# The causal mask of a gated attention moved into free rows of a bf16 product's operands

## The chip, the cores and the metric

The kernel runs on one core of a Trainium2 chip. A core has five engines with their own queues: TensorE (PE; its weight loads are shown as PEld), VectorE (DVE), ScalarE (ACT), GpSimd (POOL) and SyncE (SP, which here only issues DMAs), and 16 DMA engines. The metric is the device time of one execution in microseconds, as a median over runs. Times inside an execution come from one profiled execution and count from its first instruction.

## The reference

The input x is 8 sequences of 256 tokens with 512 features (2048 tokens); a context of the same shape is given. Two layers follow each other, each with an attention and a feed-forward part:

- layer 0: a retention-like attention over the context, then a feed-forward part whose weights are ternary and whose activations are rounded to 8 bits;
- layer 1: a matrix-LSTM attention with 16 heads of 32 features, then a mixture of 32 experts (4 of them for each token) with one shared expert.

The change is in layer 1's attention. Cut to what matters, for each batch and head:

```python
log_f_cum = concat([0, cumsum(log_sigmoid(fg))])
fg_mat    = log_f_cum - log_f_cum.T
log_D     = where(ltr, fg_mat[1:, 1:], -inf) + ig.T      # ltr: key not after query
D         = exp(log_D - max(log_D, -1))
C         = (q @ k.T / sqrt(32)) * D
Cn        = C / (maximum(abs(C.sum(-1)), exp(-max_log_D)) + 1e-6)
h         = Cn @ v                                       # then a norm per head
```

So each head needs a 256 by 256 matrix of exponentials of a sum of a term of the key and a term of the query, with everything where the key comes after the query set to zero.

## The kernel before, in words

The tokens lie in 16 tiles of 128. `layers_joined` (L1095) runs layer 0's feed-forward over the 16 tiles t and starts layer 1's attention behind it; between `layer0_attention` and it, `layer1_constants` (L654) builds constants. In both the order of PE, ACT, DVE, POOL and SP is the order in which the code emits (a manual schedule). Each engine takes its instructions in that order, and one that waits holds all behind it.

**A tile of the feed-forward** (t = 0 to 15) does: `products(t, n)` for three column blocks on PE (L1116), `silu` on ACT (L1124), `gated` on DVE (L1129), the row maximum `largest` (L1133), `shifted` (L1142), the rounding `hidden_rounded` (L1155, or L1153 on ACT) with a transposing DMA on SP (L1157), `input_rounded(t + 2)` (L1182, tile xq) with another (L1184), `output(t - 2)` (L1163), `added` (L1168) and `stats` (L127). Work of layer 1's gates (`Gates`, its generator `chain`) is placed among these by tables `steps`, `places` and `spread`: keys are (round, place in the round), values how many steps of a generator to run there.

**The exponent operands.** The gates leave, in DRAM (`parts_d`), for each row of a batch and head the key's and the query's term as three bf16 parts each, whose sum is the float32 value. For one batch b and one block k of HG = 4 heads, the exponents come from one bf16 product: its stationary operand `left` holds the key terms' three parts for the four heads in rows 0 to 11, and ones in rows 12 to 14; its moving operand `right` holds in rows 0 to 11 a pattern that picks the head, and in rows 12 to 14 the query terms' parts. So 15 rows (KR) of the 128 carry data and the others are zero. `lefts(b)` and `rights(b)` load the data rows on SP (L717, L723); there are two `left` tiles and two `right` tiles, taken in turn by batch. The second `right` is made in `second_right` (L703) in a buffer that held a weight of the feed-forward (in the profile such buffers have the name held): a memset, a copy of 12 rows by a DMA of POOL, then the loading and scaling of `ln_scale` (L711, L712). `layer1_right` (L682) writes the head pattern into the first, one block in each of tiles 2 to 5, on ACT.

**A round.** `layer1_rounds` (L686) goes through 32 blocks (b, k) in rounds n. In round n, `decays` (L736) makes the exponentials xe of block n, `weights` (L762) the product of queries and keys times xe (tile ct, one DVE instruction for two heads, L777) of block n - 1, `heads` (L783) the product with the values of block n - 2, and `back` (L801) brings block n - 3 to rows of tokens (tile hid). `decays` does this in three parts; each is one 512-column product (L749), one product that adds -1e30 to the masked places (L750), and one exponential (L754). The mask product has the identity as its stationary operand and `lateb`, a 128 by 128 triangle, as its moving one, repeated over the heads of the part:

```python
nc.tensor.matmul(pd, lhsT=lhsT, rhs=rhs, start=True, stop=False)
nc.tensor.matmul(
    pd[:, :, :P], lhsT=g.identb, rhs=lateb.unsqueeze(1).to_broadcast([P, CH // n, P]),
    start=False, stop=True,
)
nc.scalar.activation(out, pd, AF.Exp)
```

The first two parts take the first 128 keys with all 256 queries of two heads each, the third the last 128 keys with the last 128 queries of four heads. `pd` has two buffers, xe two and a third in a held buffer (`at["third"]`), which every third block takes.

**The tail of a batch** (`tail`, L885) spreads the norm of a finished batch over rounds n = 6 + 4b + r: r = 0 `scales` (L816, the maximum of |sum| and exp(-max)) and squares, r = 1 `variance` (L831, L832), r = 2 the inverse root, for b up to 5 by `rsqrt_aside` (L108: L113 and L114 on DVE, L115 to L120 on POOL), r = 3 the scaling of the heads (L838) and their addition to x (L845, L846, on POOL for b up to 5; the second half at r = 0 of the next batch), r = 5 and 6 the statistics of the new x (L127, L921, on DVE), which enter the next batch's root, r = 10 to 13 the normed rows (L864, L865) and their transposes (L875).

Of the kernel before, what the change touches and what calls it, by code (L numbers as in the profile page):

```python
# [6 lines left out]

# [645 lines left out]

def layer1_constants(g, wp):  # L654
    nc = g.nc
    g.lateb = wp.tile([P, P], BF16, tag="lateb", name="lateb")
    nc.gpsimd.memset(g.lateb, 0.0)
    nc.gpsimd.affine_select(
        out=g.lateb, in_=g.lateb, compare_op=ALU.is_ge, fill=-1e30, base=0, pattern=[[1, P]], channel_multiplier=-1
    )  # L660
    g.head = wp.tile([P, HG], F32, tag="head", name="head")
    nc.gpsimd.memset(g.head, 0.0)
    for part in range(3):
        nc.gpsimd.affine_select(
            out=g.head, in_=g.head, compare_op=ALU.not_equal, fill=1.0, base=-HG * part, pattern=[[-1, HG]],
            channel_multiplier=1,
        )

    g.left = [wp.tile([P, KD, S], BF16, tag=f"left{n}", name=f"left{n}") for n in range(2)]
    g.right = [wp.tile([P, KD, HG, S], BF16, tag="right0", name="right0")]  # L670
    for left in g.left:
        nc.gpsimd.memset(left, 0.0)
        nc.gpsimd.memset(left[:KR], 1.0)
# [7 lines left out]

def layer1_right(g, k):  # L682
    g.nc.scalar.copy(g.right[0][:, k], g.head.unsqueeze(2).to_broadcast([P, HG, S]))


def layer1_rounds(g, tc, gates, work, ps, qp):  # L686
# [4 lines left out]
    row = 2 * H1 * (HD1 + 1)  # L691
    hid_of, at = [], {}

    def opened(held):
        row = 2 * H1 * (HD1 + 1)
        first = g.ctxT[0].rearrange("p k t -> p (k t)")
        for t in (held[0][:, :row], held[0][:, row : 2 * row], first[:, :row]):
            hid_of.append(t.rearrange("p (j h d) -> p j h d", j=2, h=H1))
        gates.em = held[0][:, 2 * row : 2 * row + 2 * P].rearrange("p (n q) -> p n q", n=2)
        at["third"] = held[1][:, : HG * (S + P)].rearrange("p (r s) -> p r s", r=HG)  # L700
        at["squared"] = held[1][:, HG * (S + P) :][:, : 2 * H1 * HD1]

    def second_right():  # L703
        more = qp.tile([P, NF * D // 2], F32, tag="wq2", name="held2")
        half = KD * HG * S // 2
        nc.gpsimd.memset(more[:, :half], 0.0)
        right = more[:, :half].bitcast(BF16).rearrange("p (k r s) -> p k r s", k=KD, r=HG)
        nc.gpsimd.dma_start(out=right[: 3 * HG], in_=g.right[0][: 3 * HG])
        g.right.append(right)
        g.lns = more[:, half : half + D]  # L710
# [3 lines left out]
    def lefts(b):  # L714

        for part in range(3):
            nc.sync.dma_start(  # L717
                out=g.left[b % 2][HG * part : HG * (part + 1)],
                in_=parts_d[0, part, b * H1 : (b + 1) * H1].rearrange("(k r) s -> r k s", r=HG),
            )  # L720
# [15 lines left out]
    def decays(b, k):  # L736
# [3 lines left out]
        if (b * KD + k) % 3 < 2:  # L740
# [4 lines left out]
        def part(lhsT, rhs, late, out):  # L745
            pd = ps.tile([P, CH], F32, tag="dec", name="pd", bufs=2)
            n = rhs.shape[-1]
            pd = pd.rearrange("p (r s) -> p r s", s=n)
            nc.tensor.matmul(pd, lhsT=lhsT, rhs=rhs, start=True, stop=False)  # L749
            nc.tensor.matmul(  # L750
                pd[:, :, :P], lhsT=g.identb, rhs=lateb.unsqueeze(1).to_broadcast([P, CH // n, P]),
                start=False, stop=True,
            )
            nc.scalar.activation(out, pd, AF.Exp)  # L754

        for r in range(0, HG, 2):
            part(keys[:, :P], rows[:, r : r + 2, :], lateb, xe[:, r : r + 2, :S])
        yield xe
        part(keys[:, P:], rows[:, :, P:], lateb, xe[:, :, S:])
# [41 lines left out]
    def back(x, hid, k):  # L801
# [7 lines left out]
        nc.scalar.copy(hid[:, :, k * HG : (k + 1) * HG, :].rearrange("p j h d -> p j (h d)"), pt)  # L809
# [6 lines left out]
    def scales(b, hid):  # L816
# [3 lines left out]
        nc.scalar.activation(nm, hid[:, :, :, HD1], AF.Abs)  # L820
        nc.vector.tensor_max(nm, nm, gates.em[:, :, b * H1 : (b + 1) * H1])
# [244 lines left out]
    class Rounds:  # L1066
        def second_right(self):
            second_right()

        def lefts(self, b):  # L1070
# [782 lines left out]
```

## Time and profile before

| | us |
|---|---|
| median of 3 runs | 1052.13 (1050.63 to 1052.27) |
| the profiled execution, device time | 1052.05 |
| its span, first to last instruction | 1049.8 |
| layer 0's feed-forward, tiles 7 to 11 | about 281 to 320 |
| rounds of layer 1's attention, first to last exponent product | 358 to 492 |
| busy: PE, PEld, DVE, ACT, POOL | 997.9, 607.5, 530.7, 405.0, 397.7 |
| mean granted clock of TensorE | 0.987 |

How to read what follows. A line of an engine in order of time has the start in us, the length in us, the engine, the line of the code, the operation, output<-inputs, partitions x elements and type, and how many like it follow each other; in brackets, how long the engine had been idle before it and what ended that. Matmuls are pipelined: the next may start before the listed end of the one before. The view of windows gives a stretch's busy time for each engine. The waits give who waited for whom: total us, times, longest. The groups by tile give shortest, median and longest duration in ns.

### The profile page before, as it was taken

The page shows a single profiled execution, that of the slowest core. Times are in us where ns is not written, and L with a number is a line of the kernel's source. Part 1 is how long each engine was busy: PE and PEld are TensorE (multiplying, and loading weights), DVE is VectorE, ACT ScalarE, POOL GpSimd, SP SyncE. Part 2 cuts the span into 40 slices and gives each one's busy share as a digit, 9 for nine tenths or more (in the row PEclk, how much of TensorE's full clock was granted, in tenths as well). Part 3 has the DMA queues.
Part 4 walks back from the last instruction along what each step waited for, and adds up shares of the span by engine and source line. Part 5 has one row for each costly group of instructions (what it writes and reads, how often), then busy time and mean ns, then how long its engine had stood idle before and what let it go on. Part 6 is the DMA issues. An engine that isn't in the chain of part 4 may idle for free.

```text
span 1049.8 us, 14708 instructions
## 1 busy us (share of the span) xinstructions
PE 997.9 (95%) x5210; PEld 607.5 (58%) x5210; DVE 530.7 (51%) x1355; ACT 405.0 (39%) x692; POOL 397.7 (38%) x474
## 2 busy tenths in 40 slices
PE   6999999979999899999998989999999999999995
PEld 5766666534454355666444445556566667777773
DVE  6545566669997858887837941121212221221210
ACT  4453443447677657876421001211222223212121
POOL 0023434450000114888403044544555556545432
PEclk9999999999999999999899989999999999999998
DMA  9664433323332411231211446877877778889983
GB/s 342 228 200 146 140 102 145 101 66 57 71 62 39 90 38 48 70 127 50 76 74 51 150 145 155 211 189 179 209 195 196 209 208 227 225 228 247 235 225 49
DMA packets 101009, 152.39 MB, mean 145 GB/s; under 512 B 39577, under 2 KB 42265, under 8 KB 100893
## 3 DMA queue, kind: packets, MB, share of 16 engines
q1 hardware_dynamic: 81984, 106.78, 32.5%
q0 software_dynamic: 18944, 44.60, 19.4%
q8 instruction: 43, 0.70, 0.3%
q14 instruction: 38, 0.30, 0.1%
HBM read 110.42 MB, written 32.96 MB: 137 GB/s over the span
## 4 chain that ended last, share of the span: by engine, by line
PE 75%; DVE 12%; POOL 4%; ACT 3%; issue 2%; DMA 1%; SPq 0%; POOLq 0%; ACTq 0%; DVEq 0%
PE po L1640 14%; PE pu L1623 13%; PE pg L1623 13%; PE pw L363 5%; PE pz L398 5%; PE pt L1680 3%; PE p L1116 2%; PE pgu L988 2%; DVE am L1133 2%; DVE h L1129 2%; PE pv L297 2%; DVE ct L777 1%; PE s L340 1%; PE pq L331 1%; PE po L379 1%
## 5 line engine op out<-in xcount | busy, mean ns | idle before, releaser
L1628 DVE TENSOR_TENSOR act<-pu,sg 128x264 f32<-128x264 f32 (+22 forms) x68 | 31.8, 468 | 313.3 <-PE pu L1623 300.7
L1665 POOL DMA_INDIRECT xg<-h_d,tok_of x85 | 83.3, 980 | 199.1 <-DVE of L1675 64.3
L1684 POOL DMA_INDIRECT out_x<-eo,to x85 | 133.0, 1564 | 55.1 <-ACT eo L1722 34.4
L1640 PE MATMUL po<-w,act 128*128 128x512 f32 (+10 forms) x456 | 143.1, 489 | 0.0
L1623 PE MATMUL pg<-xT,w 128*128 128x216 f32 (+21 forms) x512 | 134.8, 406 | 0.8 <-issue 0.8
L1722 ACT ACTIVATE eo<-po,slotw 128x512 f32<-128x512 f32 (+10 forms) x114 | 65.6, 576 | 177.0 <-PE po L1640 168.4
L1623 PE MATMUL pu<-xT,w 128*128 128x216 f32 (+21 forms) x512 | 133.3, 403 | 0.0
L1623 PEld LDWEIGHTS pg<-xT,w 128*128 128x128 f32 x512 | 93.2, 190 | 33.2 <-issue 17.8
L1623 PEld LDWEIGHTS pu<-xT,w 128*128 128x128 f32 x512 | 96.8, 190 | 26.2 <-issue 5.6
L1627 ACT ACTIVATE sg<-pg 128x264 f32<-128x264 f32 (+22 forms) x68 | 28.5, 419 | 205.1 <-PE pg L1623 183.4
L1116 PE MATMUL p<-wq,xqT 128*128 128x512 bf16 (+1 forms) x384 | 81.2, 361 | 7.1 <-DVE qi L1137 6.3
L1640 PEld LDWEIGHTS po<-w,act 128*128 128x128 f32 (+10 forms) x456 | 54.1, 154 | 57.4 <-issue 47.9
L384 POOL TENSOR_TENSOR y<-y,gam 128x512 f32<-128x512 f32 x16 | 20.2, 1263 | 139.4 <-DVE y L81 139.4
L1116 PEld LDWEIGHTS <-xqT 128*128 128x128 bf16 x384 | 37.2, 98 | 49.5 <-issue 12.6
L1681 DVE TENSOR_TENSOR xT<-pt,nw 128x512 f32<-128x512 f32 (+12 forms) x85 | 51.0, 600 | 20.5 <-PE pt L1680 20.5
L398 PE MATMUL pz<-wo,wyT 128*128 128x512 f32 x128 | 59.4, 608 | 1.3 <-ACT wyT L393 1.3
L363 PE MATMUL pw<-wg,xnT 128*128 128x512 f32 x128 | 57.8, 594 | 0.0
L1680 PEld LDWEIGHTS pt<-ident,xg 128*128 128x128 f32 (+15 forms) x340 | 39.2, 140 | 23.5 <-PE po L1640 10.5
L127 DVE BATCH_NORM_STATS2 st<-x 128x6 f32<-128x512 f32 x64 | 43.9, 686 | 12.5 <-POOL x L846 6.3
L1680 PE MATMUL pt<-ident,xg 128*128 128x128 f32 (+15 forms) x340 | 47.0, 260 | 0.6 <-DVE xT L1681 0.5
L777 DVE SCALAR_TENSOR_TENSOR ct<-pqk,xe 128x768 f32<-128x768 f32 x44 | 40.0, 950 | 8.4 <-PE pqk L773 7.9
L636 POOL TENSOR_TENSOR sw<-sw 64x256 f32<-64x256 f32 x2 | 1.3, 662 | 111.8 <-ACT sw L629 111.8
(338 smaller groups left out, 1714.9 us busy)
## 6 DMA issues: line engine op xcount, KB each, us to landing
w<-in_w SPq DMA_DIRECT2D x32, 1024.0 KB
w<-in_w SPq DMA_DIRECT2D x32, 512.0 KB
wst<-in_w1T SPq DMA_DIRECT2D x8, 704.0 KB
wst<-in_w3T SPq DMA_DIRECT2D x8, 704.0 KB
wst<-in_w2T SPq DMA_DIRECT2D x6, 768.0 KB
x<-in_x SPq DMA_DIRECT2D x16, 256.0 KB
ctxT<-in_ctxT_d SPq DMA_DIRECT2D x4, 1024.0 KB
raw<-in_ctx SPq DMA_DIRECT2D x16, 256.0 KB
```

Of the source, the lines that this page charges most:

```text
L127: g.nc.vector.bn_stats(st, x)
L363: nc.tensor.matmul(pw, lhsT=xnT[c][:, k, o : o + P], rhs=wg[:, k, :], start=k == 0, stop=k == KD - 1)
L398: nc.tensor.matmul(pz[i], lhsT=wyT[i][:, k, :], rhs=wo[:, k, :], start=k == 0, stop=k == KD - 1)
L777: nc.vector.scalar_tensor_tensor(ct[:, r : r + 2, :], pqk[:, :, : S + P], 1.0 / math.sqrt(HD1), xe[:, r : r + 2, :], ALU.mult, ALU.mult,)
L1116: nc.tensor.matmul(both[:, m, : z - a], lhsT=xqT[:, k, :], rhs=w[:, k, a:z], start=k == 0, stop=k == KD - 1)
L1623: nc.tensor.matmul(pp[:, :n], lhsT=w[:, k, cols], rhs=xT[:, k, :n], start=k == 0, stop=k == KD - 1)
L1640: nc.tensor.matmul(po[h * at : h * at + n, :cols], lhsT=act[:, m, j * P : j * P + n], rhs=w[:, m, h * cols : (h + 1) * cols], start=m == 0 ...
L1665: nc.gpsimd.indirect_dma_start(out=xg[:n], out_offset=None, in_=h_d, in_offset=bass.IndirectOffsetOnAxis(ap=g.tok_of[:n, r, j : j + 1], ax ...
L1680: nc.tensor.transpose(pt[:, k, :n], xg[:n, k * P : (k + 1) * P], g.ident[:n, :n])
L1681: nc.vector.tensor_mul(xT, pt[:, :, :n], g.nw.unsqueeze(2).to_broadcast([P, KD, n]))
L1684: return nc.gpsimd.indirect_dma_start(out=g.out, out_offset=bass.IndirectOffsetOnAxis(ap=rows, axis=0), in_=eo, in_offset=None, compute_op ...
L1722: nc.scalar.activation(eo[:n, at : at + cols], po, AF.Copy, scale=w[r][:n, j : j + 1])
```

## The change

Layer 1's causal mask is no longer added by a 128-column triangle. The rows 15 to 127 of the operands, which were zero, now carry it: in `left`, row p has -1e30 in column p of each block of 128 keys; in `right`, row p has one where p is greater than the query's place in its block. Their product is -1e30 where the key is past the query, for keys from 15 on. For keys below 15 a small triangle of 14 columns is still added by a second product (14 columns for each of 4 heads). The last 128 queries against the first 128 keys need no mask: they take a third stationary operand, `open`, with zeros in rows 15 to 127, of which there are again two by batch, loaded by three more DMAs for each batch.

The rows are built by POOL instructions, three in each of the tiles 7 to 11 of the feed-forward (14 in all), each made to wait for that tile's last silu. ACT copies block 0 of `right` to blocks 1 to 3 in tiles 11 to 13, where before it wrote the pattern in tiles 2 to 5. The second `right` is made by copying rows 0 to 11 and 15 to 127 of the first; it moves to the other held buffer, and the third xe to its place.

The maximum of the norms: hid's rows get one more column; ACT copies exp(-max) into it, and one DVE reduction over pairs with absolute values takes the place of an absolute value on ACT and a maximum of two tiles on DVE. The last steps of the gates' second chain move from round 17 to 18.

```diff
-        for r in range(0, HG, 2):
-            part(keys[:, :P], rows[:, r : r + 2, :], lateb, xe[:, r : r + 2, :S])
+        part(keys[:, :P], rows[:, :, :P], xe[:, :, :P])
+        part(g.open[b % 2][:, k], rows[:, :, P:], xe[:, :, P:S], False)
         yield xe
-        part(keys[:, P:], rows[:, :, P:], lateb, xe[:, :, S:])
+        part(keys[:, P:], rows[:, :, P:], xe[:, :, S:])
...
+            nc.tensor.matmul(pd, lhsT=lhsT, rhs=rhs, start=True, stop=not masked)
+            if masked:
+                few = lateb.shape[-1]
+                nc.tensor.matmul(
+                    pd[:, :, :few], lhsT=g.identb, rhs=lateb.unsqueeze(1).to_broadcast([P, HG, few]),
+                    start=False, stop=True,
+                )
...
-        if (b * KD + k) % 3 < 2:
+        n = b * KD + k
+        if n % 3 or n == 0:
             xe = work.tile([P, HG, S + P], F32, tag="xe", name="xe")
         else:
             xe = at["third"]
...
+def operand_rows(g):
+    nc = g.nc
+    rows = g.right[0][:, 0]
+    yield nc.gpsimd.memset(rows, 0.0)
+    under = rows.rearrange("p r (j s) -> p (r j) s", s=P)
+    yield nc.gpsimd.affine_select(
+        out=under, in_=under, compare_op=ALU.is_ge, fill=1.0, base=0, pattern=[[0, 2 * HG], [1, P]], channel_multiplier=-1
+    )
+    yield nc.gpsimd.memset(rows[:KR], 0.0)
+    for part in range(3):
+        yield nc.gpsimd.affine_select(
+            out=rows, in_=rows, compare_op=ALU.not_equal, fill=1.0, base=-HG * part, pattern=[[-1, HG], [0, S]],
+            channel_multiplier=1,
+        )
+    for left in g.left:
+        yield nc.gpsimd.memset(left, 0.0)
+        blocks = left.rearrange("p k (j t) -> p (k j) t", t=P)
+        yield nc.gpsimd.affine_select(
+            out=blocks, in_=blocks, compare_op=ALU.not_equal, fill=-1e30, base=0, pattern=[[0, 2 * KD], [-1, P]],
+            channel_multiplier=1,
+        )
+        yield nc.gpsimd.memset(left[:KR], 1.0)
+    yield nc.gpsimd.memset(g.open[0], 0.0)
+    yield nc.gpsimd.memset(g.open[0][:KR], 1.0)
...
 def layer1_right(g, k):
-    g.nc.scalar.copy(g.right[0][:, k], g.head.unsqueeze(2).to_broadcast([P, HG, S]))
+    g.nc.scalar.copy(g.right[0][:, k], g.right[0][:, 0])
...
     def second_right():
-        more = qp.tile([P, NF * D // 2], F32, tag="wq2", name="held2")
         half = KD * HG * S // 2
-        nc.gpsimd.memset(more[:, :half], 0.0)
-        right = more[:, :half].bitcast(BF16).rearrange("p (k r s) -> p k r s", k=KD, r=HG)
-        nc.gpsimd.dma_start(out=right[: 3 * HG], in_=g.right[0][: 3 * HG])
+        right = at["held"][:, :half].bitcast(BF16).rearrange("p (k r s) -> p k r s", k=KD, r=HG)
+        for rows in (slice(0, 3 * HG), slice(KR, P)):
+            nc.gpsimd.dma_start(out=right[rows], in_=g.right[0][rows])
         g.right.append(right)
...
+        for part in range(3):
+            nc.sync.dma_start(
+                out=g.open[b % 2][HG * part : HG * (part + 1)],
+                in_=parts_d[0, part, b * H1 : (b + 1) * H1, :P].rearrange("(k r) s -> r k s", r=HG),
             )
...
-        nc.scalar.activation(nm, hid[:, :, :, HD1], AF.Abs)
-        nc.vector.tensor_max(nm, nm, gates.em[:, :, b * H1 : (b + 1) * H1])
+        nc.scalar.copy(hid[:, :, :, HD1 + 1], gates.em[:, :, b * H1 : (b + 1) * H1])
+        nc.vector.tensor_reduce(nm, hid[:, :, :, HD1:], AX.X, ALU.max, apply_absolute_value=True)
...
-                silu(t, 2)
+                last = silu(t, 2)
...
-                if 2 <= t < 2 + KD:
-                    layer1_right(g, t - 2)
+                if 7 <= t < 7 + 5:
+                    behind = last
+                    for ins in itertools.islice(builds, 3):
+                        tc.add_manual_dep(
+                            ins.ins, behind.ins.name,
+                            mybir.DependencyInfo(mybir.DependencyClass.Sync, mybir.DependencyReason.DATA),
+                            reason="each in its tile's time",
+                        )
+                if 10 < t < 10 + KD:
+                    layer1_right(g, t - 10)
...
-                (2, 0): [partial(output, late, "back", 1)],
+                (2, 0): [partial(output, late, "back", 1), rounds.second_right],
                 (2, 1): [partial(added, late), early],
-                (2, 2): [rounds.second_right],
+                (2, 2): [rounds.third],
...
-            spread = {..., (15, 4): 1, (17, 1): 2, (17, 4): 1}
+            spread = {..., (15, 4): 1, (18, 1): 2, (18, 4): 1}
```

`layer1_constants` loses the building of `left` (two memsets each), of the triangle's other 114 columns and of the head pattern (a memset and three selects).

## The prediction

> **What bounds the kernel now.** I read first the windows around the second layer's attention, then the waits by releaser, then single engines in order of time. A round is one pair of batch and block of four heads: 32 in all, four to a batch. PE in round 16 (start us, length us):
>
> ```profile
> 432.46 0.39 PE L749 MATMUL pd<-right,left 128*128 128x512 bf16 x1
> 432.69 0.27 PE L750 MATMUL pd<-lateb,identb 128*128 128x256 bf16 x1
> 432.80 0.38 PE L749 MATMUL pd<-right,left 128*128 128x512 bf16 x1
> 433.01 0.27 PE L750 MATMUL pd<-lateb,identb 128*128 128x256 bf16 x1
> 433.12 0.62 PE L805 MATMUL back<-turn,numT 128*128 128x132 f32 x4
> 433.65 0.38 PE L749 MATMUL pd<-right,left 128*128 128x512 bf16 x1
> 433.86 0.38 PE L750 MATMUL pd<-lateb,identb 128*128 128x512 bf16 x1
> 434.17 0.73 PE L769 MATMUL pqk<-qT,ctxT 32*128 32x256 f32 x8
> ```
>
> Lengths overlap; an instruction's cost is the distance to the next start. The three mask products (lateb) hold PE for 0.11 + 0.11 + 0.31 = 0.53 us of a round of 3.38 us. PE looks full, so it is tempting to count 0.53 thirty-two times. Windows (length, then busy us of PE, PEld, DVE, ACT, POOL, then clock and DMA) and waits (total, times, longest) say otherwise:
>
> ```profile
> 289.00:297.00 8.00, 7.38 (x39) 3.67 (x38) 7.80 (x17) 6.70 (x9) 0.00 (x0) 1.00 0.31 59
> 297.00:305.00 8.00, 8.00 (x44) 4.36 (x43) 7.79 (x20) 6.26 (x9) 0.00 (x0) 1.00 0.38 73
> 369.00:398.00 29.00, 27.54 (x256) 15.46 (x258) 17.40 (x37) 17.28 (x36) 4.53 (x4) 1.00 0.19 52
> 398.00:424.00 26.00, 24.76 (x278) 15.33 (x278) 25.14 (x41) 19.27 (x45) 13.48 (x22) 1.00 0.10 28
> ...
> DVE st L127 <- POOL x L846: 6.3, 5, 1.8
> POOL var L115 <- DVE rsq L113: 5.4, 5, 1.9
> ```
>
> Tiles 7 to 10 of the feed-forward (281 to 313 us) leave DVE no gap while POOL is empty. Rounds 2 to 6 (369 to 398) are PE's: DVE has 17.40 of 29. Rounds 7 to 12 are DVE's (25.14 of 26). From 424 to 497 a loop rules, one turn a batch: POOL takes the root, scales the heads and adds them to x (L115 to L846, 9.6 to 10.2 us in a row); DVE waits for that x in all five batches, then does L127, L831, a ct, L127 and L113 (5.2 us); POOL waits for L113. That makes 14.8 to 15.4; the turns start at 424.61, 439.41, 454.86, 470.72 and 486.95. There is no PE time in it; PE's four rounds need 13.5, with two transposed tiles at 0.44 each 14.4.
>
> **The change part by part.**
>
> *Masks on PE.* Three mask products a round go, two of 56 columns come. By the rows a column costs (0.379 - 0.273)/256 us, so 56 cost 0.02; but the weights of the open product behind the first take 0.097 (PEld row of L750). Between 0.02 and 0.11 for it I take 0.10, nearest the weight row; for the one ahead of pqk, between 0.10 and 0.31, 0.20. A round saves 0.53 - 0.30 = 0.23 (0.11 to 0.41), 7.4 in all rounds. It reaches the end only in rounds 2 to 6, and of these five about one is lost to waits inside (num for DVE's qT 0.89, back for numT 0.41): 4 x 0.23 = **-0.9** (-0.4 to -1.6). Rounds 0 and 1 wait for DMA and ACT; from 7 on DVE and the loop cover the masks. ACT's exponents keep count and size; block 2 writes xe again after block 0's ct (done 370.60, exponent at 370.51): 0.1, in the rounding.
>
> *Maximum of the norms.* ACT's Abs (0.25) becomes a copy of as many elements: nothing. DVE's maximum reads two tiles and took 0.18 beside an idle POOL:
>
> ```profile
> 416.63 1.06 DVE L821 TENSOR_TENSOR nm<-nm,held 128x32 f32<-128x32 f32 x1
> 430.20 1.49 DVE L821 TENSOR_TENSOR nm<-nm,held 128x32 f32<-128x32 f32 x1
> ...
> 429.74 1.91 POOL L838 TENSOR_TENSOR held<-held,rsq 128x1024 f32<-128x1024 f32 x1
> ```
>
> The second ends (430.20 + 1.49) as POOL's L838 ends (431.65). Reductions show no such stretching: L831 takes 1.19 beside POOL and 1.21 without. Only 416.63 lies in the DVE-bound part; there the next stats start 0.45 after POOL's x was ready, so **-0.4** (0 to -0.9). At 430.20 DVE waits for POOL afterwards anyway.
>
> *Operand rows on POOL, tiles 7 to 11.* This is where I expect the loss. 14 instructions, three after each tile's last silu, two in tile 11. Rows of before:
>
> ```profile
> L672 POOL MEMSET left<- x2: 946/954/962, 228.6 to 233.0; 128x1024 bf16 x2
> ...
> L658 POOL TENSOR_SCALAR_AFFINE_SELECT lateb<-lateb x1: 297/297/297, 229.5 to 229.5; 128x128 bf16<-128x128 bf16 x1
> ...
> 294.37 0.42 DVE L1182 TENSOR_SCALAR xq<-xn 128x512 bf16<-128x512 f32 x1
> ```
>
> A select of 4 columns takes 0.19 and of 128 0.30: 0.86 ns a column, so 1024 take 1.07; a memset 0.95. POOL's time itself is free. But silu ends at 285.66, 294.00, 301.83 and 309.83, and xq starts 0.06 to 1.2 us after that, just inside the three. If it is held to the end of the POOL instruction that runs: tile 7 1.1, tile 8 0.75, tile 9 0.9, tile 10 0.85 and 1.05 more for L104 (two inputs, beside the select): 4.7. If only selects hold, 2.3 (0.5 + 0.75 + 0 + 1.05). No row shows DVE beside a memset or select of this size, so 0 to 4.7; L821, L921 (0.62 beside POOL's L865, else 0.17) and L636 (1.24 beside L838, else 0.42) are the nearest rows and all hold: between the two cases **+3.3**. DVE has no gap there, so it passes to the end one for one.
>
> [...]
>
> *Copy in round 2.* The memset of 1.81 goes; a copy of 113 rows of 8 KB joins that of 12 (1.02 MB together). It now goes into the buffer of w3, free when tile 15's products end at 355.5, and POOL has nothing before it: it starts some 17 us earlier than before (memset at 372.55), beside the transposing DMA of hq (issued 356.81), for which PE waits 1.61 us until 360.38. The 16 DMA engines are full from 358 to 361 (windows: share 1.05, 1.01, 0.86 at 205, 180 and 297 GB/s). At these rates the copy takes 3.4 to 5 us. If they share, hq lands up to 3.5 later; 0.56 of it is slack (PE then waits for ACT). 0 to 3, I take **+1.2**. Rights of batch 1 no longer wait on SP for POOL's memset (7.6 us); not needed before 381. The ln_scale multiply (1.52 on POOL at 380.39) comes earlier too, perhaps beside DVE's root chain (363.8 to 365.1), whose end ACT awaits: 0 to 1.5, **+0.4**. The open memsets and DMA issues on POOL (0.6 each) stand in front of nothing urgent.
>
> *SP.* 24 more DMAs of 0.3. In tile 15 three stand ahead of the hq transpose; SP had 0.8 free there: 0.1 at most. Later lefts go out at 425.3, 440.3, 454.6, 469.6 for rounds that start at 432.5 (16), 447.7, 462.7, 478.1: 6 us to spare. Nothing.
>
> *ACT.* Four casts of 1.03 go from tiles 2 to 5, three copies come to tiles 11 to 13. ACT idles after each of them (2.48, 1.23 and 3.24 us); without that cover they'd cost 3. POOL's memsets at 228 to 235 go; that path is DMA Wif (3.71). Nothing. The second gates' last steps move from round 17 to 18: PE's wait of 0.48 for POOL goes, off the loop.
>
> **Sum** against the profiled execution (1052.05; span 1049.8 and 2.25 around it; 0.08 below the median): -0.9 - 0.4 + 3.3 + 1.2 + 0.4 = +3.6, **1055.7**.
>
> **The rivals.**
>
> 1. POOL's rows slip between DVE's instructions and the copy yields to hq: the costs are 0, -1.3 remains, 1050.8. For it: memsets read nothing, and no row shows them holding DVE. Against: xq's place just behind silu. No change that can be told.
> 2. Faster: PE sets the loop's rounds after all and the masks pay in all 32: -7.4 - 0.4 + 4.9 = -2.9, 1049.2 (1044.3 with no costs). It decides once PE rather than POOL's x is what DVE waits for, that is, if the turn gets shorter than 14.8. For it: 72.11 of 76 us busy on PE from 424 to 500. Against: the two waits above, ten times in five batches.
> 3. Much slower: selects take what POOL's two-input rows do (1.18 for 512, so 2.4), and hq is held 3.5: +4.7 + 3.0 + 1.5 - 0.4 = +8.8, 1060.9.
> 4. The short products save nothing beyond 0.11 a round: the masks' term is -0.4, the sum +4.1; inside the forecast.
>
> **How the numbers follow.** This kernel's runs can't tell less than about 0.2%, 2.1 us, from no change. Forecast 0.52, rival 3 0.10 (both slower), rival 1 0.22 (same), rival 2 0.16 (faster). The range leaves out rival 2's end and the top of rival 3: 1050.0 to 1060.0; the forecast's own range is 1054.2 to 1058.5.
>
> **What would show it.** Right: xq at 0.6 to 1.5 us in tiles 7 to 10, the ends of these tiles 2 to 5 us later; hq's landing later than 3.5 us after issue; nm near 0.2 always; round time 3.15 on PE in rounds 2 to 6 but turns of 14.8 to 16 as before, with PE idle before pqk. Wrong: xq at 0.42 throughout; turns under 14.5.

## The result, and the profile after

| | before | after |
|---|---|---|
| median, us | 1052.20 (4 runs, 1050.63 to 1052.50) | 1065.09 (4 runs, 1062.00 to 1065.67) |
| ratio | | 1.0121, 95% [1.0108, 1.0134] |
| profiled execution, its span | 1052.05, 1049.8 | 1064.74, 1062.9 |

The change costs 12.9 us. I had predicted 3.6 us slower and a range up to 1060.0: the direction was right, the size was not, and the time lies outside the range.

To see where the 13.1 us between the two spans went, I cut both at the same work: the products py of the tiles on PE (the first is tile 0's, which runs in the time of tile 2 and which the expectations call "py of tile 2"; the last two are those of tiles 14 and 15) and POOL's first instruction of each root (L115, now L116).

| stretch, us | before | after | difference |
|---|---|---|---|
| start to the first py | 246.21 | 245.48 | -0.7 |
| first py to py of tile 13 (POOL's rows) | 109.03 | 112.40 | +3.4 |
| py of tile 13 to py of tile 14 (hq) | 5.14 | 15.01 | +9.9 |
| py of tile 14 to py of tile 15 | 9.57 | 9.99 | +0.4 |
| py of tile 15 to the first root (rounds 2 to 6) | 38.67 | 37.93 | -0.7 |
| first root to last root (five turns) | 78.33 | 78.19 | -0.1 |
| last root to the end | 562.85 | 563.90 | +1.0 |

The first and the last row are scatter: among the kernels run below that are the same up to there, the first py starts between 245.1 and 247.6, and the last stretch takes between 561.5 and 564.5, although none of them changes its code.

**The copy.** PE around the large row, in order of time (start, length, line, count; in brackets the idle time before and what ended it), before and after:

```profile
357.96 0.38 PE L749 MATMUL pd<-right,left 128*128 128x512 bf16 x1 [0.19 <-DMA right<-parts_d]
...
360.38 2.55 PE L1163 MATMUL py<-wq,hq 128*128 128x512 bf16 x11 [1.61 <-DMA hq<-hq]
```

```profile
357.88 2.54 PE L1201 MATMUL py<-wq,hq 128*128 128x512 bf16 x11
362.70 0.38 PE L782 MATMUL pd<-right,left 128*128 128x512 bf16 x1 [2.29 <-DMA right<-parts_d]
362.92 0.19 PE L785 MATMUL pd<-lateb,identb 128*128 128x56 bf16 x1
362.94 0.42 PE L782 MATMUL pd<-right,open 128*128 128x512 bf16 x1
...
372.89 4.46 PE L1201 MATMUL py<-wq,hq 128*128 128x512 bf16 x11 [9.53 <-DMA hq<-hq]
```

PE waits 9.53 us for the transposed hq of tile 14, where it waited 1.61 before, and 2.29 us for the query rows in `right`, where it waited 0.19: 7.9 and 2.1 us more, the 9.9 of the table. POOL had issued the copy of 12 rows (L735) at 358.34 and that of 113 rows at 358.94, SP the transposing DMA at 359.45, as the queues show; its issue alone takes 4.48 us, and that of tile 15's 3.74, against 1.39 to 1.42 before:

```profile
358.94 0.56 POOL L735 DMA_DIRECT2D held<-right  x1
```

```profile
359.04 0.24 SPq L757 DMA_DIRECT2D right<-parts_d  x1
359.45 4.48 SPq L1195 DMA_TRANSPOSE hq<-hq  x1
364.02 2.40 SPq L766 DMA_DIRECT2D raw<-vc_d  x2
366.55 3.74 SPq L1195 DMA_TRANSPOSE hq<-hq  x1
```

In windows of 2 us (length, busy us of PE, PEld, DVE, ACT, POOL, then granted clock, DMA share, GB/s):

```profile
360.00:362.00 2.00, 0.41 (x2) 0.10 (x1) 1.97 (x2) 0.00 (x0) 1.09 (x3) 1.00 1.09 181
362.00:364.00 2.00, 0.66 (x3) 0.19 (x2) 1.90 (x6) 1.38 (x1) 0.00 (x0) 0.79 0.96 190
364.00:366.00 2.00, 0.00 (x0) 0.00 (x0) 1.79 (x10) 1.97 (x4) 0.00 (x0) 0.50 0.84 117
366.00:368.00 2.00, 0.00 (x0) 0.00 (x0) 1.56 (x8) 0.57 (x2) 0.00 (x0) 0.50 1.12 115
368.00:370.00 2.00, 0.00 (x0) 0.00 (x0) 0.00 (x0) 0.00 (x0) 0.00 (x0) 0.50 1.30 102
370.00:372.00 2.00, 0.00 (x0) 0.00 (x0) 0.00 (x0) 0.00 (x0) 0.00 (x0) 0.50 0.91 158
```

The DMA engines are busy throughout but move 102 to 190 GB/s, where I had reckoned with 205 to 297; from 368 to 372 no engine of the core has anything to do. And PE's clock falls to 0.50 while it idles, so that the eleven products of py take 4.46 us in place of 2.55 when they come.

**POOL's rows.** DVE and POOL in tile 9, after:

```profile
302.73 0.92 DVE L1220 TENSOR_SCALAR xq<-xn 128x512 bf16<-128x512 f32 x1
303.57 0.60 DVE L1167 SCALAR_TENSOR_TENSOR h<-p,s,sg 128x384 f32<-128x384 f32 x1
304.21 1.62 DVE L1171 TENSOR_REDUCE am<-h 128x1 f32<-128x1408 f32 x1
...
302.42 0.96 POOL L696 MEMSET left<- 128x1024 bf16 x1 [4.74 <-ACT sg L1162]
303.44 1.15 POOL L698 TENSOR_SCALAR_AFFINE_SELECT left<-left 128x1024 bf16<-128x1024 bf16 x1
304.65 0.94 POOL L702 MEMSET left<- 15x1024 bf16 x1
```

xq (0.42 otherwise) starts inside the memset and ends 0.27 us after it; the product and the reduction that follow have their usual length beside a select and a memset. The same in tile 8 (xq 1.10, beside selects) and tile 10 (L102 0.82 for 0.15, xq 1.15); in tile 7 it is nb (1.05 for 0.16) that is held, and xq slips through.

**Masks and maximum.** A round on PE, after:

```profile
445.27 0.38 PE L782 MATMUL pd<-right,left 128*128 128x512 bf16 x1
445.49 0.19 PE L785 MATMUL pd<-lateb,identb 128*128 128x56 bf16 x1
445.61 0.73 PE L804 MATMUL pqk<-qT,ctxT 32*128 32x256 f32 x8
...
447.28 0.39 PE L782 MATMUL pd<-right,left 128*128 128x512 bf16 x1
447.51 0.19 PE L785 MATMUL pd<-lateb,identb 128*128 128x56 bf16 x1
447.54 0.38 PE L782 MATMUL pd<-right,open 128*128 128x512 bf16 x1
447.89 0.72 PE L840 MATMUL back<-turn,numT 128*128 128x132 f32 x4
448.45 0.38 PE L782 MATMUL pd<-right,left 128*128 128x512 bf16 x1
```

From one third part (445.27) to the next (448.45) it is 3.18 us; the short products hold PE for 0.12 ahead of pqk and 0.03 ahead of open. The open product itself holds PE for 0.35 up to back, where the product in its place before (432.80 in the prediction's lines) has 0.21. So all products into pd take 0.95 us of this round and 1.18 of round 16 before, 0.23 less. Why the open product is dearer is not shown; with the long masks (e14 below) it holds PE for 0.22 again. But the turns of the five batches take 15.70, 14.81, 15.48, 15.93 and 16.27 us, before 15.99, 14.80, 15.45, 15.86 and 16.23. Only the first is shorter. The maximum's reduction takes the same time in every batch now (ns, shortest, median, longest; the maximum before had 180, 194, 1492).

```profile
L856 DVE TENSOR_REDUCE nm<-held x6: 207/210/221, 411.9 to 519.6; 128x32 f32<-128x64 f32 x6
```

### The profile page after: what moved, and what is told of

It is laid out like the page before. It is cut to its first block, busy times and chain, and to the rows that moved or that the text cites. A ratio compares the mean times of both kernels' runs of the same rounds, so it can differ in the third digit from the quotient of the medians.

```text
span 1062.9 us, 14688 instructions
## 1 busy us (share of the span) xinstructions
PE 994.1 (94%) x5178; PEld 606.3 (57%) x5178; DVE 533.7 (50%) x1355; ACT 401.1 (38%) x691; POOL 407.5 (38%) x482
## 4 chain that ended last, share of the span: by engine, by line
PE 74%; DVE 12%; POOL 4%; ACT 4%; issue 2%; DMA 2%; SPq 0%; POOLq 0%; ACTq 0%; DVEq 0%
PE po L1687 14%; PE pg L1670 13%; PE pu L1670 13%; PE pw L364 5%; PE pz L399 5%; PE pt L1727 3%; PE p L1154 2%; PE pgu L1023 2%; PE py L1201 2%; PE pv L298 2%; DVE ct L812 2%; DVE h L1167 1%; DVE am L1171 1%; PE s L341 1%; PE pq L332 1%
## 5 line engine op out<-in xcount | busy, mean ns | idle before, releaser
L1201 PE MATMUL py<-wq,hq 128*128 128x512 bf16 x176 | 42.5, 392 | 9.7 <-DMA hq<-hq 9.5
```

The lines of the kernel that those rows point to most:

```text
L1201: nc.tensor.matmul(py[t], lhsT=hqT[t][0][:, f, :], rhs=w2[:, f, :], start=f == 0, stop=f == NF - 1)
```

## The experiments

All start from the changed kernel but one, which starts from the kernel before. "Ratio" is to the kernel before, with its 95% interval; the stretches are those of the table above.

| kernel | us | ratio | rows: first py to py 13 | hq: py 13 to py 14 | py 14 to py 15 | py 15 to root | PE's wait for hq |
|---|---|---|---|---|---|---|---|
| before | 1052.2 | | 109.0 | 5.1 | 9.6 | 38.7 | 1.6 |
| after | 1065.1 | 1.0121 | 112.4 | 15.0 | 10.0 | 37.9 | 9.5 |
| e1 copy late | 1057.3 | 1.0039 [1.0027, 1.0052] | 112.4 | 5.3 | 10.2 | 40.1 | 1.1 |
| e2 rows early | 1066.7 | 1.0125 [1.0104, 1.0146] | 109.0 | 14.7 | 10.6 | 38.0 | 9.2 |
| e3 both | 1058.2 | 1.0054 [1.0034, 1.0075] | 109.0 | 5.3 | 9.8 | 38.6 | 1.1 |
| e4 113 rows late | 1057.7 | 1.0045 [1.0031, 1.0059] | 112.4 | 7.0 | 9.8 | 38.0 | 1.8 |
| e5 pieces | 1057.5 | 1.0050 [1.0034, 1.0067] | 112.4 | 7.7 | 10.1 | 38.0 | 3.7 |
| e13 large pieces first | 1063.2 | 1.0119 [1.0096, 1.0142] | 112.4 | 13.6 | 10.2 | 37.9 | 8.7 |
| e10 112 rows | 1060.7 | 1.0087 [1.0066, 1.0107] | 112.4 | 9.9 | 10.1 | 37.9 | 4.9 |
| e6 copy on SP | 1080.6 | 1.0268 [1.0251, 1.0285] | 112.4 | 6.6 | 9.6 | 62.3 | 2.5 |
| e7 SP, rows behind xq | 1077.1 | 1.0240 [1.0225, 1.0254] | 109.0 | 6.4 | 9.7 | 61.7 | 2.3 |
| e9 SP, 112 rows, behind xq | 1053.2 | 1.0006 [0.9994, 1.0017] | 109.0 | 6.7 | 10.9 | 38.1 | 2.7 |
| e11 112 behind py 14, behind xq | 1053.2 | 1.0015 [1.0001, 1.0028] | 109.0 | 5.2 | 11.2 | 38.2 | 1.1 |
| e12 the same, memsets behind py 15 | 1052.4 | 1.0000 [0.9988, 1.0011] | 109.0 | 5.2 | 9.4 | 39.5 | 1.1 |
| e14 the same, full masks back | 1050.6 | 0.9991 [0.9980, 1.0003] | 109.0 | 5.2 | 9.5 | 38.8 | 0.7 |
| e8 before, a mask twice | 1054.1 | 1.0015 [1.0004, 1.0025] | 109.0 | 5.2 | 9.7 | 39.6 | 1.8 |

**Which part is the loss (e1 to e4).** e1 holds the copies until tile 15's last product of w2 (`g.last_py`, kept in `output`); e2 builds the rows in `layer1_constants`; e3 does both; e4 holds only the copy of 113 rows.

```diff
         for rows in (slice(0, 3 * HG), slice(KR, P)):
-            nc.gpsimd.dma_start(out=right[rows], in_=g.right[0][rows])
+            ins = nc.gpsimd.dma_start(out=right[rows], in_=g.right[0][rows])
+            tc.add_manual_dep(
+                ins.ins, g.last_py.ins.name,
...
```

> The two copies into the second right wait for the last product of w2 (py of tile 15); everything else as in the changed kernel (1065.1 us). Theory 1, the copy beside the transposing DMAs of hq is the loss: hq is issued by SP in 1.4 us again (4.48 and 3.74 in the changed kernel), PE waits for it 1.6 us (9.5), TensorE's clock stays at 1.00 from 360 to 376 (0.50 there), time 1065.1 - 10 = 1055 (1053.5 to 1056.5). Theory 2, the three loads of open or the load of ln_scale, which start at the same place, hold hq: the wait stays near 9.5 us and the time at 1063 to 1066. Theory 3, the copy is missed by rounds 4 to 7, which need the second right from about 384 on: the wait moves there, time 1056 to 1062.

> The 14 instructions that build the operand rows run on POOL before the feed-forward's tiles, where the kernel before had its own, with no wait for a silu; the copy stays where the changed kernel has it. Theory 1, they held DVE in tiles 7 to 10: xq back from 0.92 to 1.15 us to 0.42, py of tile 13 2.6 us earlier against the same start, time 1065.1 - 2.6 = 1062.5 (1061.5 to 1064), or less gain if the rows hold DVE in tiles 0 and 1 instead, which leave it 0.5 us each. Rival, DVE's longer tiles were covered by PE: time within 1 us of 1065.1.

```diff
+    for _ in operand_rows(g):
+        pass
     g.turn = wp.tile([P, HG, HD1 + 1], F32, tag="turn", name="turn")
...
-                if 7 <= t < 7 + 5:
-                    behind = last
...
```

> Late copy and early rows together. If the two causes are the whole loss and independent: 1065.1 - 10 - 2.6 = 1052.5 (1050.5 to 1054), not to be told from the kernel before (1052.2): the masks and the maximum bring nothing that reaches the end, 0.4 to 1.3 us at most by my terms. If the masks pay in all 32 rounds once the copy is out of the way: under 1049.

> The copy of 12 rows (96 KB) and the load of ln_scale (256 KB) keep their early place on POOL's queue; only the copy of 113 rows (904 KB) waits for the last product of w2. Theory 1, the size is what holds hq: nearly as the late copy, 1055 to 1057, PE's wait for hq 1.6 to 3 us. Rival, anything on POOL's queue ahead of the transposing DMA holds it, whatever its size: PE's wait stays over 6 us, 1060 to 1065.

```diff
-        for rows in (slice(0, 3 * HG), slice(KR, P)):
-            nc.gpsimd.dma_start(out=right[rows], in_=g.right[0][rows])
+        nc.gpsimd.dma_start(out=right[: 3 * HG], in_=g.right[0][: 3 * HG])
...
         nc.gpsimd.dma_start(out=g.lns, in_=g.ln_scale.partition_broadcast(P))
+        ins = nc.gpsimd.dma_start(out=right[KR:], in_=g.right[0][KR:])
+        tc.add_manual_dep(
+            ins.ins, g.last_py.ins.name,
...
```

e1 settles the large row: with the copy out of the way hq is issued in 1.41 and 1.39 us, and the stretch is 5.3 us again; the three loads of open ahead of it stand where they stood, and so they were not the cause of the wait for hq. e4 agrees, though its time lies 0.7 us above what I had given it: it was the 904 KB; the 12 rows and ln_scale in their early place leave a wait of 1.8 us. But e1 gains 7.8, not 10, because theory 3 also holds in part: its copy runs from 376 on, and so do the memsets of the second open and the load of ln_scale, which stand behind it on POOL; SP's loads for batch 1 wait for the memsets, PE waits 1.5 us for these loads, and py of tile 15 to the root takes 40.1 us, 2.2 more than in the changed kernel. Behind that wait the clock is at 0.50 from 385.6 to 389.1; e3 has the wait (1.4) without the fall, and takes 38.6. In e4, where only the 113 rows come late, this is not so (38.0). e3 has no loss for the rows in tiles 7 to 11, but pays for them ahead of the first py as e2 does, and comes to 1058.2 and not 1052.5.

e2 went against my expectation. The 3.4 us of tiles 7 to 11 go, and 5.6 come back ahead of the first py. There the rows run on POOL without a pause, and DVE has to wait through several of them. DVE and POOL of e2:

```profile
232.88 3.39 DVE L1223 TENSOR_SCALAR xq<-xn 128x512 bf16<-128x512 f32 x1 [0.16 <-ACT xn L1183]
...
233.34 0.23 POOL L544 COPY sw<-ident 128x64 f32<-128x64 f32 x1
233.52 1.09 POOL L701 TENSOR_SCALAR_AFFINE_SELECT left<-left 128x1024 bf16<-128x1024 bf16 x1
234.58 0.39 POOL L1612 TENSOR_TENSOR gw<-gw,nw 128x128 f32<-128x128 f32 x1
234.94 1.05 POOL L694 TENSOR_SCALAR_AFFINE_SELECT right<-right 128x1024 bf16<-128x1024 bf16 x1
```

An xq of 0.42 us ends only when this chain lets go, at 236.27. A little later an operation on one column (L1188, 0.14 otherwise) takes 2.38 beside a memset and two selects.

**What the copy does to hq (e5, e13, e10).** e5 splits the copy into eight DMAs with packets of 2 KB, e13 also exchanges the two slices, so that the pieces of 113 rows go first, e10 leaves the packets but copies 1 and 112 rows for 113.

```diff
         for rows in (slice(0, 3 * HG), slice(KR, P)):
-            nc.gpsimd.dma_start(out=right[rows], in_=g.right[0][rows])
+            for k in range(KD):
+                nc.gpsimd.dma_start(out=right[rows, k], in_=g.right[0][rows, k])
```

> The changed kernel with its copy where it was, but as eight DMAs of one block each (packets of 2 KB in place of 8 KB). If long packets are what the transposing DMA waits behind, hq comes back earlier: PE's wait 3 to 6 us in place of 9.5, time 1058 to 1062. If it is the total of bytes that the DMA engines have to move first, or POOL's queue as such: PE's wait 8 to 11 us and 1064 to 1067, the issues on POOL (0.6 us each) moving little.

> The copy in pieces of 2 KB packets, the pieces of 113 rows now issued ahead of those of 12 rows, so that the first two stand ahead of hq's transposing DMA (before, only pieces of 12 rows did). If the packet's length is what cost, PE's wait for hq stays near the 3.7 us of the pieces, 1056 to 1059. If it is what stands ahead of hq in bytes, the wait comes back to 6 to 9 us, 1060 to 1065.

> The changed kernel with the copy at its place on POOL's queue, 8 KB packets, as 12, 1 and 112 rows instead of 12 and 113. Theory 1 (packets of 8 KB stand ahead of the transposing DMA's on every engine): as the changed kernel, PE's wait for hq 8 to 10 us, 1063 to 1066. Theory 2 (the uneven 113 rows load a few engines with most of the copy, and the transposing DMA, which needs all 16, waits for these): wait 3 to 5 us, 1056 to 1060.

```diff
-        for rows in (slice(0, 3 * HG), slice(KR, P)):
+        for rows in (slice(0, 3 * HG), slice(KR, KR + 1), slice(KR + 1, P)):
             nc.gpsimd.dma_start(out=right[rows], in_=g.right[0][rows])
```

e5 alone would have been read as "long packets hold the transpose". It was not so: in e5 the first large piece was issued 1.0 us after the start of hq's issue, and the pieces of 12 rows stood ahead of hq or beside it. With the first two large pieces ahead of it (e13; the third comes 0.03 us after it) and packets as short, PE waits 8.7 us again. So it is what stands ahead of the transposing DMA, and not the packet's length. PE's waits by releaser (total, times, longest), e13 first, then e10:

```profile
PE py L1202 <- DMA hq<-hq: 8.7, 1, 8.7
```

```profile
PE py L1201 <- DMA hq<-hq: 4.9, 1, 4.9
```

e10 looks as if the 113 rows cost 9.5 us of waiting for hq and 112 only 4.9. But it changes two things. The DMA of one row takes its turn on POOL's queue, so that the 112 rows are issued 0.02 us after hq, and not 0.51 ahead of it as the 113 were. POOL and SP of e10:

```profile
359.08 0.55 POOL L735 DMA_DIRECT2D held<-right  x1
```

```profile
359.06 2.85 SPq L1195 DMA_TRANSPOSE hq<-hq  x1
```

So e10 doesn't tell the number of rows from the order, and no other run does for POOL's queue. That a transposing DMA takes the engines all together the kernel before shows: from 343 to 345, where only those of hq and xq run, the DMA share is 1.09 and they move 204 to 212 GB/s. For the number of rows speaks that in e11 and e12 (below) 112 rows are issued 2.5 and 1.7 us ahead of tile 15's hq, and PE runs that tile's py 6.9 and 5.8 us after hq's issue began, without a wait for hq; in the changed kernel tile 14's py came 13.4 us after it.

**The copy on SP, and the rows behind xq (e6, e7, e9).** e6 issues the copy on SP behind hq; e7 also moves the rows to pairs behind each xq of tiles 4 to 10; e9 is e7 with 1 and 112 rows for 113.

```diff
-            nc.gpsimd.dma_start(out=right[rows], in_=g.right[0][rows])
+            nc.sync.dma_start(out=right[rows], in_=g.right[0][rows])
```

> The two copies go to SP's queue, issued behind the last transposing DMA of hq (at about 368) instead of on POOL; nothing else. The copy is then neither ahead of hq nor, as in the late copy, ahead of batch 1's operand rows: hq is issued in 1.4 us, PE waits for it 1 to 2 us, and the wait of 1.5 us for batch 1's rows goes. 1054 to 1056.5 (before + 3.4 for the rows on POOL - 0.7 - 0.5). If it still delays batch 1's rows, which follow on the same queue: 1057 to 1060.

> As the copy on SP, and the 14 instructions on POOL come two by two in tiles 4 to 10, each pair behind that tile's xq instead of behind a silu: DVE then has 2.2 us of a product with PSUM and a reduction, which no row shows held. If holding xq was what the rows cost (3.4 us from py of tile 2 to py of tile 13): 109.0 us there again as in the kernel before (112.4 in the changed one), and a time 3 us below the copy on SP, 1050.5 to 1053. Rival, POOL holds the products and reductions too: no gain.

```diff
-                if 7 <= t < 7 + 5:
-                    behind = last
-                    for ins in itertools.islice(builds, 3):
...
                 if t + 2 < NT:
                     input_rounded(t + 2)
+                if 4 <= t < 4 + 7:
+                    behind = g.last_xq
+                    for ins in itertools.islice(builds, 2):
...
```

> As the copy on SP with the rows behind xq (1077.1), but the 113 rows are copied as 1 and 112. In the copy on SP the 904 KB moved at 26 to 31 GB/s with a DMA share of 0.07, about one engine of 16, for some 33 us. Theory 1: 113 rows can't be dealt out evenly to 16 engines and go to one; 112 are 16 times 7 and go at 200 GB/s or more, in about 5 us: PE's wait of 22.6 us for batch 1's rows goes, 1077 - 25 = 1051 to 1053. Rival: SP's queue takes any copy from SBUF to SBUF on one engine, then 1076 to 1078 again.

e6 missed by 24 us, and told most. Windows of e6 while the copy runs, then PE's longest wait:

```profile
376.00:384.00 8.00, 7.44 (x69) 4.66 (x72) 6.50 (x15) 6.06 (x12) 0.00 (x0) 1.00 0.07 28
392.00:400.00 8.00, 0.00 (x0) 0.00 (x0) 0.00 (x0) 0.00 (x0) 0.00 (x0) 0.50 0.07 29
```

```profile
PE pd L782 <- DMA left<-parts_d: 22.6, 1, 22.6
```

A DMA share of 0.07 is about one engine of 16, and it moves 28 GB/s; everything that SP issues behind the copy waits for it. With 112 rows (e9, issued at 368.1) the windows of 2 us from 368 to 372 show 171 and 291 GB/s at a DMA share of 0.87 and 0.95, and of the 1077 us of e7, which differs from e9 in this alone, 24 are gone. So on SP's queue 113 rows went at about the pace of one engine and 112 did not; why, and where other numbers of rows fall, no run here shows. On POOL's queue it was otherwise: in e3 the window from 381 to 385 shows a DMA share of 0.93 and 233 GB/s (other loads among them), and PE reads the second `right` from 388.14 on, 9.2 us after the issue of its 113 rows, too early for one engine at 28 GB/s (33 us). e9 ends just above what I expected (1053.2 for 1053 at most), with 2.7 us of waiting for hq.

The rows behind xq cost nothing, in e7 as in e9, e11 and e12: 109.0 us, as in the kernel before. e7 is 3.5 us below e6, as expected, and misses its range for e6's reason. DVE and POOL of e7:

```profile
293.70 0.42 DVE L1220 TENSOR_SCALAR xq<-xn 128x512 bf16<-128x512 f32 x1
294.03 0.61 DVE L1167 SCALAR_TENSOR_TENSOR h<-p,s,sg 128x384 f32<-128x384 f32 x1
294.68 1.62 DVE L1171 TENSOR_REDUCE am<-h 128x1 f32<-128x1408 f32 x1
...
294.24 0.94 POOL L702 MEMSET left<- 15x1024 bf16 x1 [5.67 <-DVE xq L1220]
295.12 0.94 POOL L696 MEMSET left<- 128x1024 bf16 x1
```

**Both repaired (e11, e12).** Rows behind xq, and the copy on POOL as 12, 1 and 112 rows, held until the first product of py of tile 14, when that tile's hq has landed (`g.first_py`, by tile); e12 also holds the memsets of the second open, and with them the load of ln_scale, until the first product of tile 15.

```diff
+            tc.add_manual_dep(
+                ins.ins, g.first_py[NT - 2].ins.name,
...
-        opened_rows(g, 1)
+        ins = opened_rows(g, 1)
+        tc.add_manual_dep(
+            ins.ins, g.first_py[NT - 1].ins.name,
...
```

> The rows behind xq, and the copy (12, 1 and 112 rows) on POOL's queue, held until the first product of w2 of tile 14, that is until hq of tile 14 has landed; hq of tile 15, issued some 3 us later, has about 2 us to spare. If all that was lost were those two places: nothing lost for the rows (3.4), PE's wait for hq 1.6 to 2.5 us, the masks' 0.7 in rounds 2 to 6 kept: 1050.5 to 1052.5, the same as the kernel before or 1 to 2 us faster. If the copy holds tile 15's hq by more than its slack: 1053 to 1058.

> As behind py14 (rows behind xq; the copy as 12, 1 and 112 rows held until tile 14's first product of w2), and what follows the copy on POOL (the two memsets of the second open, the load and the scaling of ln_scale) waits for tile 15's first product of w2. Behind py14 these memsets held DVE: L95 0.52 us for 0.16 and hq 1.32 for 0.89, 0.8 in the chain to nb for which ACT and PE wait. If that is what is left: nb at 0.8 us less after py of tile 14 than there, 1052.3 (1051 to 1053), not to be told from the kernel before; the masks' 0.7 would be what is gained at most. If the late memsets hold up batch 1's open rows on SP instead: 1053 to 1056.

e11 comes to 1053.2, above the 1052.5 that I had expected at most without a new loss; e12 can't be told from the kernel before (1.0000). In e11 the memsets at 361.9 to 363.0 hold DVE's L95 (0.52) and hq (1.32 for 0.89), and the clock is at 0.50 from 367.7 to 371.1; in e12 neither is so. But then the masks' gain ought to show, and from py of tile 14 to the root e12 takes 48.9 us, the kernel before 48.2. In the profile the loss is one of clock. Windows of 4 us around round 4 of e12:

```profile
378.00:382.00 4.00, 2.33 (x28) 1.26 (x25) 3.16 (x8) 3.00 (x6) 0.00 (x0) 1.00 0.07 17
382.00:386.00 4.00, 4.00 (x30) 3.17 (x29) 0.89 (x2) 1.70 (x4) 0.00 (x0) 0.57 0.02 4
```

PE has 2.33 us of work in 4, and in the next 4 the granted clock is 0.57. Little work in a window is not enough for that: e10 has 2.32 us in its window of the same round (386 to 390), and the clock stays at 1.00; the last section says what differs. In the kernel before it has 3.11 us there, and the clock stays at 1.00. Over 12 runs the mean granted clock of e12 is 0.9834 (0.982 to 0.985), that of the 17 runs of the kernel before beside them 0.9857 (0.984 to 0.987).

**The masks' work put back (e14).** e12 with the whole triangle in the mask products again, so that PE has as much to do in a round as in the kernel before (products into pd of 1.17 us; that is 0.23 more than in e12 and not 0.43, as the expectation has it):

```diff
-    g.lateb = wp.tile([P, KR - 1], BF16, tag="lateb", name="lateb")
+    g.lateb = wp.tile([P, P], BF16, tag="lateb", name="lateb")
...
-        out=g.lateb, in_=g.lateb, compare_op=ALU.is_ge, fill=-1e30, base=0, pattern=[[1, KR - 1]], channel_multiplier=-1
+        out=g.lateb, in_=g.lateb, compare_op=ALU.is_ge, fill=-1e30, base=0, pattern=[[1, P]], channel_multiplier=-1
```

> The repaired version (rows behind xq, copy behind py of tile 14, memsets behind py of tile 15), but with the full triangle of 128 columns in the mask products, so that PE's masks take 0.43 us more in every round again, as much as in the kernel before; the result is the same, since the triangle is added where the operands' rows mask already. In the repaired version PE's clock fell to 0.53 and 0.62 from 382 to 386, and its mean granted clock is 0.9834 over 12 runs, against 0.986 in the kernel before and in the one with a mask twice. [...]

The same windows of e14:

```profile
378.00:382.00 4.00, 2.74 (x39) 1.39 (x31) 3.39 (x10) 2.70 (x6) 0.00 (x0) 1.00 0.06 17
382.00:386.00 4.00, 3.91 (x47) 2.79 (x48) 2.03 (x3) 2.48 (x6) 0.00 (x0) 1.00 0.01 4
```

With more work for PE the clock stays at 1.00 in the profile, its mean over 12 runs is 0.9863 (0.984 to 0.987) where e12 has 0.9834, and py of tile 14 to the root takes 48.3 us for 48.9. The mean counts every fall: of the two stretches at 0.50 that e12's profile has beyond e14's, one lies here and one near 220 us, ahead of the tiles. The time, 1050.6, is the lowest of all medians here, but 0.9991 with an interval that reaches over 1 is not told from the kernel before, and it overlaps e12's. So in the repaired version the masks' 14 columns in place of 128 bring nothing that can be told: in e12's profile PE loses by a slower clock what it saves in rounds 2 to 6.

**What a mask costs (e8).** The kernel before, with the third part's mask product issued twice:

```diff
-            nc.tensor.matmul(
-                pd[:, :, :P], lhsT=g.identb, rhs=lateb.unsqueeze(1).to_broadcast([P, CH // n, P]),
-                start=False, stop=True,
-            )
+            times = 2 if n == P else 1
+            for m in range(times):
+                nc.tensor.matmul(
+                    pd[:, :, :P], lhsT=g.identb, rhs=lateb.unsqueeze(1).to_broadcast([P, CH // n, P]),
+                    start=False, stop=m == times - 1,
+                )
```

> The kernel before, with the mask product of the third part (512 columns, 0.31 us) issued twice in each of the 32 rounds: 9.9 us more of PE, the result unchanged. By my forecast PE sets the end only in rounds 2 to 6: 4 x 0.31 = +1.2, with up to 0.5 a batch more where four rounds of PE (13.5 + 1.2, and 0.9 of transposes) come up to a turn of 14.8 to 16: 1053 to 1056. Rival, PE sets the rounds throughout, so that masks taken out would have paid in full: +9.9, 1062.

9.9 us more of PE cost 1.6 us (0.4 to 2.6). In the profile rounds 2 to 6 are 0.9 longer and the five turns together 0.3 (78.66 for 78.33). PE's time in the masks is thus nearly free from round 7 on, and taking it away brings nearly nothing there: 0.2 us in the first turn (15.70 in e12, 15.89 in e14).

## Why the prediction was wrong, by its steps

- *Masks on PE*, -0.9: measured -0.7 between py of tile 15 and the first root; e4, e5, e10 and e13 have the same 37.9 to 38.0 there. In e12, where PE doesn't wait long for hq, the clock takes it back, which I had not reckoned with. The step that PE's time matters in rounds 2 to 6 alone is right in the main, and e8 confirms it from the other side; it left out the first turn (0.2 us in e14 against e12, and 0.2 in e8 against the kernel before). A round saves 0.23 as I had it, but by luck: the short products hold PE for 0.03 ahead of open, where I took 0.10, and 0.12 ahead of pqk, where I took 0.20, and the open product for 0.14 more than the one it replaces, which I had not counted. Some three rounds of the saving reach the end and not four.
- *Maximum of the norms*, -0.4: only the first turn is shorter, as the step said, but of its 0.3 us the long masks of e14, which has the new maximum, take 0.2 back (15.99 before, 15.89 in e14, 15.70 in e12). So some 0.1 is the maximum's, by one profile each.
- *Operand rows on POOL*, +3.3: measured +3.4, and the hits in the trace (0.9 + 0.7 + 0.5 + 0.7 + 0.7) add up to 3.5. That memsets hold xq too, which I left between the cases, is now seen twice (0.92 us at 302.73 and 1.15 at 312.98, for 0.42). The sum stays under its 4.7 because single holds are shorter than I worked out, above all xq in tile 9 (0.5 for 0.9) and L102 in tile 10 (0.7 for 1.05); in tile 7 it was nb, and not xq, that was caught. That 3.3, a value between two cases, came so near is in part luck.
- *Copy in round 2* and *ln_scale multiply*, +1.2 and +0.4: this is the step that failed. It measured +9.9, and +0.4 up to tile 15's py. The place was right: the copy starts at 358, beside the transposing DMA of hq, and hq is late. The size was wrong in "At these rates the copy takes 3.4 to 5 us. If they share, hq lands up to 3.5 later". The rates were those of other DMAs in that window. What ran was the 113 rows, the transposes, the raw loads and ln_scale together, at 102 to 190 GB/s with the engines' share near 1, for 14 us; of the 9.9 us, 7.9 are the wait for hq and 2.1 that for `right` ahead of it. The wait for hq follows the order of issue: 9.5 and 8.7 us with large pieces ahead of hq (the changed kernel, e13), 4.9 with them issued 0.02 us after it (e10), 3.7 with them 1.0 us after it (e5), 1.1 with none (e1). Why these transfers together move so little, and what part the uneven 113 rows have in it, stays open. A second price was not in the working at all: PE's clock at 0.50 after the wait, 1.9 us in py of tile 14. The stretch up to tile 15's py hardly shows it (+0.4); I take it that DVE and ACT, which idle from 368 to 372, had got ahead during the wait.
- *SP*, nothing: right lands later behind the loads of open (PE waits 1.0 for it in e1, where the copy is away, 0.19 before), but the wait for hq behind it shrinks from 1.6 to 1.1; 0.1 in all, as said. Beside the copy PE waits 2.29 for it; that is counted with the copy.
- *ACT*, nothing: right; nothing shows there.
- Rival 3, the much slower case, had hq held, as it was, and capped it at 3.5 us; its selects of 2.4 us took 1.1 to 1.3. Rival 1, costs of 0, falls with the rows' 3.4, and rival 2, PE setting every round, with e8. The range ended at 1060 because no row of the trace before showed a transposing DMA beside a large copy, and I took a bound from bandwidth where the order of issue decided as well.

## What to carry to other kernels

When a change starts a large transfer earlier, ask what will be issued behind it on the same DMA engines: the transposing DMA paid for what was issued ahead of it (PE waited 9.5 and 8.7 us for it with large pieces ahead, 1.1 with none), and paid more than the 3.5 us at most that I had estimated from a share of the bandwidth. On SP's queue, look at the number of rows too: 113 rows moved at 25 to 31 GB/s, a DMA share of about one engine of 16 (e6), and 112 at 171 and 291 GB/s (e9). POOL's work was free beside DVE where DVE did a reduction or read PSUM (in e7 1.62 and 0.61 us beside memsets, their usual lengths, and 109.0 us for the stretch as before), so hang it on the DVE instruction that opens such a stretch. Before taking work off an engine, double it once and see what the end does (9.9 us more of PE cost 1.6 in e8), and on PE look at the granted clock afterwards (0.9834 in e12, 0.9857 in the kernel before).

## What the runs showed that I had not expected

- One DMA of 113 rows by 8 KB within SBUF on SP's queue moved at 25 to 31 GB/s with a DMA share of 0.06 to 0.08 for about 35 us (e6); with 112 rows the windows show 171 and 291 GB/s (e9). All SP's later loads waited.
- POOL instructions that follow each other closely hold one DVE instruction through several of them: 3.39 us for 0.42, 2.38 for 0.14 (e2).
- PE with less to do was no faster: mean granted clock 0.9834 without the full masks (e12), 0.9863 with them (e14), and 0.9 us between the two medians' ratios to the kernel before, in favour of the kernel with more work (the intervals overlap).
- PE's clock fell to 0.50 after short waits too, and not always: in e1 and e3 PE waits the same 1.0 and 1.1 us ahead of py of tile 14, and py takes 2.55 us in e1 and 4.23 in e3. The traces show a pattern. The clock stays at 0.50 for 3.41 us or a whole multiple of it (13.65 in the changed kernel). Lay windows of 3.41 us along a trace so that they end where the clock falls (13 profiles, 240 to 495 us, windows at a clock of 1.00): all 14 windows in which PE idled for 1.9 us or more were followed by 0.50, 4 of the 19 with 1.39 to 1.9 us of idling, and 2 of the 894 with less. So it matters where a wait lies. In e3 both waits fall into one window (2.11 us idle, 362.88 to 366.29), in e1 into two (there the clock falls later, at 368.57, behind a window with 1.59 us of idling). In round 4 of e12 waits of 1.07 and 0.60 us share a window, in e10 they lie in two; in e14 they are 0.94 and 0.42, 1.36 together. This was read from the traces afterwards; no run was made to test it. The windows that a fall followed were not all idle: in some of them PE was busy for up to 1.5 us, and in e12 for 1.74.
